# A row-LSTM kernel: 64-row matmul pieces, and gates to output in two parts

## The chip, the cores and the metric

The kernel runs on one core of one Trainium2 chip. The metric is the device time of one launch in microseconds. A profiled execution gives a page and a trace of every instruction; durations below come from it. The engines are called PE or TensorE (matmuls; PEld are its weight loads), DVE or VectorE, ACT or ScalarE, POOL or GpSimd, and SP or SyncE, which here issues all DMAs.

## The reference

The input is x of shape (8, 96, 128, 128): 8 images, 96 channels, 128 rows, 128 pixels in a row. It is group-normalised over 32 groups, and a row LSTM runs over it from the first row to the last. For each row, a masked three-tap convolution of the normalised row and a three-tap convolution of the previous row's h make four gates:

```python
def step(carry, row_in):
    h, c = carry
    ss = conv(h, W_ss, taps=3) + b_ss          # 96 -> 384 channels
    gates = ss + row_in                        # row_in: masked conv of the normalised row
    g5 = gates.reshape(B, 3, 4, Oc, Wd)        # Oc = 32
    f, i, o = (sigmoid(g5[:, :, k].reshape(B, O, Wd)) for k in (0, 1, 2))
    g = tanh(g5[:, :, 3].reshape(B, O, Wd))
    c_new = f * c + i * g
    h_new = o * tanh(c_new)
    return (h_new, c_new), h_new
```

The output is x plus all h. Everything is float32. Row r + 1 needs h of row r, so the 128 rows are a chain.

## The kernel before, in words

**Halves and half-steps.** The 8 images are two halves of four (`NH = 2`, `BH = 4`). A half-step n is one row of one half: `row, s = divmod(n, 2)`, 256 half-steps in all. The two halves alternate, so that one half's gates can be worked on while the other half's matmuls run. A name with ' belongs to half-step n - 1, with + to n + 1, with * to n + 2 and, in the kernel after, with '' to n - 2. S, F and D are named by the half-step whose h they read; what they make is used two half-steps later.

**Even and odd pixels.** A row of 128 pixels is held as 64 even and 64 odd ones (`J = 64`), each with padding. A three-tap convolution makes an even and an odd output from them with four products in place of six: the moving operands are a sum `vs` (S, line 499), a difference `vf` (F, line 503) and a pair of shifted differences `vd` (D, line 507), each 128 partitions x 256 elements (4 images x 64 pixels), made from `hx`. Partitions 0 to 95 of `hx` hold h, 96 to 127 the last 32 normalised input channels. The 64 other input channels come as `xs`, made ahead by GpSimd (`own_image`, lines 297, 315 and 316), and they are stored twice, on partitions 0 to 63 and on 64 to 127.

**Gate tiles.** The 384 output channels are three tiles A, B, C of 128, each in a PSUM bank of 512 elements: the first 256 are one half, the last 256 the other. Tile A's rows 0 to 95 are the forget gate, B's the input gate, C's the output gate; rows 96 to 127 of all three are g. For each tile the products are:

- 1 with vs into the first half, 2 with vf into the second, and the own products P (first half) and Q (second), with xs.
- then `copy` (cp: first half plus bias to SBUF, called m), `even` (lo: first half = m + second half, line 442) and `odd` (hi: second half = m - second half, line 446).
- then 0 with vd into the first half, 3 with vd into the second, and the own product E into the first.

Products 0, 1, 2, 3 contract over 128 rows, P, Q, E over 64. Before the change `own` puts P, Q and E of tile A on the lower 64 rows of the array, of B on the upper, and of C on either by half, so that neighbours can run together.

**Gates.** `tanh` (ta, ACT, line 449) of g's rows, `sigmoid` (si, ACT, line 456), `forget` (fg: f x c, DVE, line 461), `gated` (gt: i x g, line 465), `cell` (ce: line 474), `cell_tanh` (th, ACT, line 479), `output` (ou: o x tanh(c) into hx of the next row, line 486). From hx come S, F (DVE) and D (POOL) for the same half's next row. `residual` (re, POOL, line 525) adds h to x in place.

**Order.** PE, ACT, DVE and POOL are scheduled by hand (`manual_schedule`): each engine runs its instructions in the order in which the program writes them, and waits for others by semaphores. The steady order is the string `PERIOD` with the products `PRODUCTS` in place of X, played by `do` for n = 3 to 255. One half-step has 12 whole products and, in turn, 8 or 10 own ones.

**Blocks.** Rows are loaded in blocks of four. `finish(n)` comes after re': GpSimd's preparation of coming rows (`work`: one `own_image`, and none, one or two images of `normalise_shared`, line 297), and at a block's last row the store of the block and the loads of the block after the next, all on SP's queue. Before the steady part, some 137 us compute the group statistics and the first row.

Of the kernel before, what the change touches and what calls it, by code (L numbers as in the profile page):

```python
# [8 lines left out]
AF = mybir.ActivationFunctionType  # L9
# [12 lines left out]
def kernel(  # L22
# [32 lines left out]
    nc = tc.nc  # L55
    B, C, H, W = x.shape
    P = 128
    NH = 2
    BH = B // NH
# [4 lines left out]
    C2 = 64  # L64
# [21 lines left out]
    wt = [tap[1], wm[:, 0, :], wm[:, 1, :], tap[2]]  # L86
    wo = [wx[:, 0, :], wx[:, 1, :], tap[3]]
# [73 lines left out]
    E = mybir.EngineType  # L161
# [64 lines left out]
    class Scale:  # L226


        def __init__(self, s, lo, hi, banks=None):
            n, self.name = hi - lo, f"{s}_{lo}"  # L230
            self.st, self.rstd, self.nmr = (
                st[s][:, lo:hi], rstd[s][:, :, lo:hi], nmr[s][:, :, lo:hi]
            )


            self.first, at = banks is None, 0 if banks is None else 3 * BH
            self.banks = banks or [bank(f"{name}{self.name}") for name in ("dm", "pv")]
            self.dm, self.pv = (
                own[:, at : at + i * n].rearrange("p (i b) -> p i b", i=i)
                for own, i in zip(self.banks, (3, 2))  # L240
            )
            self.pm = self.dm[:, 1:3, :]
            self.q, self.t, self.minus = (
                const.tile([P, *shape], F32, name=f"{name}{self.name}")
                for name, shape in (("q", [n]), ("t", [2, n]), ("minus", [2, n]))
            )
            for i in range(2):
                self.mm(self.pv[:, i, :], i, eps[:, 0:n], start=self.first and i == 0)
# [107 lines left out]
    last = NT * NH - 1  # L356
    order = {"A": 0, "B": 1, "C": 2}

    def gt(n, s, row, shape=(C, 2 * HB)):
        return g_pool.tile(list(shape), F32, tag=n, name=f"{n}_{s}_{row}")  # L360

    class HalfStep:


        def __init__(self, n):
            self.n, (self.row, self.s) = n, divmod(n, NH)
            self.ps, self.m1, self.moving, self.done, self.gates = {}, {}, {}, set(), None
            self.started, self.images = set(), {}
            self.hx = hx[self.s][self.row // R % 2][:, self.row % R]
            self.xs = xs[self.s][self.row // R % 2][:, self.row % R]  # L370
            self.c = cs[self.s].rearrange("p t b j -> p (t b j)")
# [14 lines left out]
        def mm(self, a, half, weights, rhs, rows=slice(0, P)):  # L386
            self.take_bank(a)
            new = a not in self.started
            self.started.add(a)

            lo, hi = self.images.get(a, (0, BH))
            cols = slice(lo * J, hi * J)
            nc.tensor.matmul(  # L393
                self.ps[a][:, bass.ts(half, HB)][:, cols],
                weights[rows, bass.ts(a, P)],
                rhs[rows, cols],
                start=new,
                stop=False,
                skip_group_check=True,
            )  # L400

        def own(self, a, i):

            low = a == order["A"] or (a == order["C"] and (self.s == 0 or (self.n, i) == (1, 2)))
            rhs = self.xs[:, i].rearrange("p b j -> p (b j)")
            self.mm(a, i % 2, wo[i], rhs, slice(0, C2) if low else slice(C2, P))

        def p_(self, a):
            self.own(a, 0)
# [5 lines left out]
        def t_(self, a):  # L415
            if 2 * self.row + self.s == last:
                self.mm(a, 0, wh, self.xs[:, 2].rearrange("p b j -> p (b j)"))
            else:
                self.own(a, 2)

        def m1_(self, a):
            self.mm(a, 0, wt[1], self.moving["vs"][:, 0])

        def m2_(self, a):
            self.mm(a, 1, wt[2], self.moving["vf"][:, 0])

        def m0_(self, a):
            self.mm(a, 0, wt[0], self.moving["vd"][:, 1])

        def m3_(self, a):  # L430
            self.mm(a, 1, wt[3], self.moving["vd"][:, 0])

        def copy(self, a):
            self.m1[a] = self.tile(f"m{a}", (P, HB))
            m1, column = self.ps[a][:, 0:HB], bias[:, a : a + 1]
            if a == order["A"] and self.n not in (0, 2):
                nc.vector.tensor_scalar(self.m1[a], m1, column, None, ALU.add)
            else:
                nc.scalar.activation(self.m1[a], m1, AF.Identity, bias=column)  # L439

        def even(self, a):
            nc.vector.tensor_add(self.ps[a][:, 0:HB], self.m1[a], self.ps[a][:, HB:])  # L442

        def odd(self, a):
            hi = self.ps[a][:, HB:]
            nc.vector.tensor_sub(hi, self.m1[a], hi)  # L446

        def tanh(self, a):
            nc.scalar.activation(self.g[a * 32 : (a + 1) * 32], self.ps[a][C:P], AF.Tanh)  # L449


        def sigmoid(self, a):
# [7 lines left out]
            if self.row > 0:  # L460
                nc.vector.tensor_mul(f, f, self.c)  # L461

        def gated(self):
            to = self.g if self.row > 0 else self.c
            nc.vector.tensor_mul(to, self.ps[1][0:C], self.g)


        def part(self, ap, lo, hi):
            return ap.rearrange("p (t b j) -> p t b j", t=2, b=BH)[:, :, lo:hi]

        def cell(self, lo=0, hi=BH):
            if self.row > 0:
                c, f, g = (self.part(ap, lo, hi) for ap in (self.c, self.ps[0][0:C], self.g))
                nc.vector.tensor_add(c, f, g)  # L474

        def cell_tanh(self, lo=0, hi=BH):
            if lo == 0:
                self.th = self.tile("th")
            nc.scalar.activation(self.part(self.th, lo, hi), self.part(self.c, lo, hi), AF.Tanh)  # L479

        def output(self, lo=0, hi=BH):
            s, row = self.s, self.row
            nxt = hx[s][(row + 1) // R % 2][0:C, (row + 1) % R]
            self.h = strided(nxt[:, 0, 0, :], 0, [(BH * JP + 1, 2), (JP, BH), (1, J)])
            o, th = (self.part(ap, lo, hi) for ap in (self.ps[2][0:C], self.th))
            nc.vector.tensor_mul(self.h[:, :, lo:hi], o, th)  # L486


        def operand(self, name, parts=1):
# [65 lines left out]
    def work(n):  # L555
        if n < len(FIRST):
            return FIRST[n]
        row, s = divmod(n, NH)
        k, r = divmod(row, R)
        parts = []  # L560
        if r == R - 1 and k + 2 < NB:
            parts.append((own_image, s, k + 2, 0))
        elif r < R - 1 and k + 1 < NB:
            parts.append((own_image, s, k + 1, r + 1))
        if k + 1 < NB:
            parts += shared(s, k + 1, *SHARED[r])
        if r == R - 2 and k + 2 < NB:
            parts.append((load_rows, s, k + 2))
        return parts

    def finish(n):
        for part, *args in work(n):
            part(*args)
        row, s = divmod(n, NH)
        k, r = divmod(row, R)
        if r == R - 1:
            store(s, k, R - 1 if k + 1 == NB else 0, R)
            if k + 2 < NB:
                load(s, k + 2)
        elif r == R - 2 and k + 1 == NB:  # L580
            store(s, k, 0, R - 1)
# [2 lines left out]


    PERIOD = (
        "2A 1A siB' fg' 2B taB' cpA 1B loA 3C' cpB hiA 0C' loB 1C taC' hiB 2C siC' 0A gt'",
        "3A cpC ce' 0B loC th' hiC", "X", "ou' F' S' D' re'", "3B taA siA",
    )
    PRODUCTS = (  # L590
        "P+A P+B Q+A Q+B P+C P*A Q+C EA EB EC",
        "Q+A P+B P+C Q+B Q+C EB EA EC",
    )
    PARTS = {
        "P": "p_", "Q": "q_", "E": "t_", "1": "m1_", "2": "m2_", "0": "m0_", "3": "m3_",
        "cp": "copy", "lo": "even", "hi": "odd", "ta": "tanh", "si": "sigmoid",
# [7 lines left out]
            steps[n] = HalfStep(n)  # L604
        return steps[n]

    def do(n, names):

        for name in names.split():
            at = n  # L610
            for mark, offset in (("'", -1), ("+", 1), ("*", 2)):
                if mark in name:
                    at, name = n + offset, name.replace(mark, "")
            tile_ = name[-1] if name[-1] in order else ""
            part = name[: len(name) - len(tile_)]

            if part in ("S", "F", "D"):
                at += NH
            if not 0 <= at <= last:
                continue  # L620
            step = half_step(at)
            if name not in step.done:
                step.done.add(name)
                getattr(step, PARTS[part])(*([order[tile_]] if tile_ else []))

# [117 lines left out]
    n = m = 0  # L745
    for b in range(B):
# [7 lines left out]
        for k in range(QW // CH):  # L754
# [11 lines left out]
            if alone:  # L766
                i = list(shares).index(k)
# [60 lines left out]
    finish(0)  # L828
    do(1, "gt th 0+A 3+A 0+B 3+B 0+C 3+C ou F S D re")
    finish(1)  # L830
    do(2, "taA siA P+C P*A Q+C")
    for n in range(3, last + 1):
        for names in PERIOD if n < last else PERIOD[:1]:
            do(n, PRODUCTS[n % 2] if names == "X" else names)
            if "re'" in names.split():
                finish(n - 1)
    do(last, "3A EA cpC ce' taA siA 0B 3B EB loC hiC th' siB taB fg ou' re'")
    finish(last - 1)
    do(last, "0C 3C EC taC siC gt")
    step, halves = half_step(last), [(0, BH // 2), (BH // 2, BH)]  # L840
    for at in halves:
        step.cell(*at)
# [60 lines left out]
```

## Time and profile before

| | |
|---|---|
| median of 3 runs | 2062.37 us (2062.25 to 2062.47) |
| span of the profiled execution | 2059.9 us |
| granted TensorE clock, mean | 0.997 |
| MATMUL instructions (two to each float32 product) | 10888 |
| TensorE busy from 160 to 2040 us | 1880.00 of 1880 us |
| VectorE, ScalarE, GpSimd busy in that stretch | 1554.98, 1247.29, 1380.49 us |

A matmul's record lasts longer than its share of the array: records overlap, so the rate is read from start to start. In a line of the timeline the numbers are start and duration in us; a line that ends in x6 holds six instructions of one kind. In the view of waits the numbers are us in total, times, and the longest. In the view of a tile they are ns (least, median, most) and the first and last start in us. The small difference between the median of the runs and the span, 2.5 us, lies around the profiled instructions.

### The profile page before, as it was taken

Reading aid. Unit: us, or ns where it says so; the run is one execution under the profiler, and the core shown is the slowest. Engines: PE = TensorE matmul, PEld = TensorE weight load, DVE = VectorE, ACT = ScalarE, POOL = GpSimd, SP = SyncE. Lnnn points to the kernel's source line nnn. Section 1 sums busy time; section 2 is a strip of 40 time slices with the busy share of each in tenths; the row PEclk is TensorE's granted clock in tenths of the full one; section 3 lists DMA queues with packets and bytes.
Section 4 is the critical chain, followed back from the end, with each engine's and each line's share of the span. In section 5 each row is a group of like instructions: output and inputs, shape, how many; then the busy total and the mean of one; then the engine's idle time right before and its main releaser. Section 6 shows DMA issues by size and latency. Waiting matters only on the chain.

```text
span 2059.9 us, 31445 instructions
## 1 busy us (share of the span) xinstructions
PE 1961.9 (95%) x10888; PEld 1597.5 (78%) x10888; DVE 1675.9 (81%) x3489; ACT 1363.7 (66%) x2403; POOL 1449.6 (70%) x1652
## 2 busy tenths in 40 slices
PE   0399999999999999999999999999999999999998
PEld 0278888888888888888888888888888888888886
DVE  5778888888888888888888888888888888888887
ACT  4776666666666666666666666666666666666666
POOL 3358777777777777777777777777777777777762
PEclk9999999999999999999999999999999999999999
DMA  9994333344433334443333443333444333344411
GB/s 381 424 309 109 91 84 89 97 113 113 107 74 85 88 99 113 113 103 75 86 88 101 113 113 100 73 90 87 104 113 113 99 74 87 88 106 113 113 31 32
DMA packets 103326, 236.26 MB, mean 115 GB/s; under 512 B 5953, under 2 KB 8897, under 8 KB 97281
## 3 DMA queue, kind: packets, MB, share of 16 engines
q1 hardware_dynamic: 103168, 234.25, 41.8%
q8 instruction: 88, 1.44, 0.3%
q14 instruction: 70, 0.57, 0.1%
HBM read 183.90 MB, written 50.33 MB: 114 GB/s over the span
## 4 chain that ended last, share of the span: by engine, by line
PE 93%; DMA 3%; DVE 2%; ACT 1%; POOL 0%; issue 0%; SPq 0%; DVEq 0%; POOLq 0%
PE ps L393 93%; DMA xs<-in_x_dram 3%; DVE bst L771 1%; POOL xw L297 0%; POOL xs L315 0%; POOL xs L316 0%; ACT piece L295 0%; SPq L759 0%; ACT piece L216 0%; ACT xs L216 0%; ACT xs L217 0%; ACT piece L217 0%; ACT g L449 0%; DVE st L677 0%; ACT th L479 0%
## 5 line engine op out<-in xcount | busy, mean ns | idle before, releaser
L393 PE MATMUL ps<-vd,wl 128*128 128x256 f32 x3072 | 814.3, 388 | 0.1
L449 ACT ACTIVATE g<-ps 32x512 f32<-32x512 f32 x768 | 454.3, 592 | 450.5 <-PE ps L393 442.4
L393 PEld LDWEIGHTS ps<-vd,wl 128*128 128x128 f32 x3072 | 562.4, 190 | 151.3 <-issue 84.7
L507 POOL TENSOR_TENSOR vd<-hx 128x512 f32<-128x512 f32 x257 | 266.5, 1037 | 459.0 <-DVE vs L499 457.8
L393 PE MATMUL ps<-xs,wx 64*128 64x256 f32 x3080 | 459.9, 394 | 11.0 <-POOL xs L315 11.0
L393 PE MATMUL ps<-vs,wm 128*128 128x256 f32 x1540 | 460.6, 381 | 4.0 <-POOL vs L499 4.0
L393 PE MATMUL ps<-vf,wm 128*128 128x256 f32 x1540 | 460.4, 381 | 0.0
L456 ACT ACTIVATE ps<-ps 96x512 f32<-96x512 f32 x766 | 417.7, 572 | 16.1
L393 PEld LDWEIGHTS ps<-xs,wx 64*128 64x128 f32 x3080 | 323.9, 187 | 119.7 <-issue 83.9
L461 DVE TENSOR_TENSOR ps<-ps,c 96x512 f32<-96x512 f32 x254 | 176.6, 695 | 259.4 <-ACT ps L456 259.4
L446 DVE TENSOR_TENSOR ps<-m,ps 128x256 f32<-128x256 f32 x768 | 329.1, 429 | 27.3 <-PE ps L393 1.2
L525 POOL TENSOR_TENSOR x<-x,hx 96x512 f32<-96x512 f32 x255 | 330.5, 1296 | 5.7 <-DVE hx L486 5.7
L442 DVE TENSOR_TENSOR ps<-m,ps 128x256 f32<-128x256 f32 x768 | 324.8, 423 | 9.7 <-ACT m L439 0.9
L393 PEld LDWEIGHTS ps<-vs,wm 128*128 128x128 f32 x1540 | 293.6, 191 | 45.9 <-POOL vs L499 5.0
L393 PEld LDWEIGHTS ps<-vf,wm 128*128 128x128 f32 x1540 | 293.9, 191 | 41.1 <-POOL vf L503 0.5
L439 ACT ACTIVATE m<-ps,wl 128x256 f32<-128x256 f32 x514 | 243.9, 475 | 74.8 <-PE ps L393 61.5
L316 POOL TENSOR_TENSOR xs<-xw 128x512 f32<-128x512 f32 (+1 forms) x254 | 270.4, 1064 | 0.0
L393 PE MATMUL ps<-xs,wt 64*128 64x256 f32 x1530 | 264.6, 377 | 0.0
L479 ACT ACTIVATE th<-c 96x512 f32<-96x512 f32 (+1 forms) x257 | 161.4, 628 | 104.8 <-DVE c L474 103.8
L297 POOL TENSOR_SCALAR hx<-x,rstd,nmr 32x512 f32<-32x512 f32 (+1 forms) x252 | 204.7, 812 | 25.9
L297 POOL TENSOR_SCALAR xw<-xr,rstd,nmr 128x512 f32<-128x512 f32 x252 | 204.8, 813 | 8.1 <-DVE nmr L289 6.5
L393 PEld LDWEIGHTS ps<-xs,wt 64*128 64x128 f32 x1530 | 195.0, 187 | 18.1 <-issue 0.7
(91 smaller groups left out, 1295.2 us busy)
## 6 DMA issues: line engine op xcount, KB each, us to landing
xr<-in_x_dram SPq DMA_DIRECT2D x124, 512.0 KB, 6.7
x<-in_x_dram SPq DMA_DIRECT2D x63, 768.0 KB, 5.9
out_dram<-x SPq DMA_DIRECT2D x62, 768.0 KB, 4.9
xs<-in_x_dram SPq DMA_DIRECT2D x30, 1024.0 KB, 12.3
piece<-in_x_dram SPq DMA_DIRECT2D x16, 1024.0 KB, 12.3
x<-in_x_dram SPq DMA_DIRECT2D x62, 256.0 KB, 3.2
xs<-in_x_dram SPq DMA_DIRECT2D x4, 512.0 KB, 8.3
out_dram<-x SPq DMA_DIRECT2D x2, 576.0 KB, 3.8
```

The source lines that it names most:

```text
L297: engine.tensor_scalar(dst, src, scale, shift, ALU.mult, ALU.add)
L316: nc.gpsimd.tensor_sub(differences, strided(xw[:, 0, :], 0, [(W + 1, n), (J, 2), (1, J)]), strided(xw[:, 0, :], J + 1, [(W + 1, n), (0, 2) ...
L393: nc.tensor.matmul(self.ps[a][:, bass.ts(half, HB)][:, cols], weights[rows, bass.ts(a, P)], rhs[rows, cols], start=new, stop=False, skip_g ...
L439: nc.scalar.activation(self.m1[a], m1, AF.Identity, bias=column)
L442: nc.vector.tensor_add(self.ps[a][:, 0:HB], self.m1[a], self.ps[a][:, HB:])
L446: nc.vector.tensor_sub(hi, self.m1[a], hi)
L449: nc.scalar.activation(self.g[a * 32 : (a + 1) * 32], self.ps[a][C:P], AF.Tanh)
L456: nc.scalar.activation(gate, gate, AF.Sigmoid)
L461: nc.vector.tensor_mul(f, f, self.c)
L479: nc.scalar.activation(self.part(self.th, lo, hi), self.part(self.c, lo, hi), AF.Tanh)
L507: diff = nc.gpsimd.tensor_sub(self.operand("vd", 2)[:, :, lo:hi], strided(h, 1, [(BH * JP - 1, 2), (JP, hi - lo), (1, J)]), strided(h, 0, ...
L525: (nc.gpsimd if 2 * row + s < last else nc.vector).tensor_add(xo, xo, self.h)
```

## The change

It has four parts.

1. In the steady part each of the products 0, 1, 2, 3 is issued as two pieces of 64 rows, and P, Q and E as one piece each. `Lanes` gives every piece the lower or the upper 64 rows of the array: the two pieces of a product take different ones, and otherwise the lanes alternate. Where a piece goes to a bank whose last product ran on the other rows, `Lanes.wait` makes TensorE wait first for that product's end. In `PERIOD` a product's name stands twice where it has two pieces.
2. tanh of C, gated, cell, cell_tanh and output are issued in two parts, first the odd pixels (b), then the even ones (a).
3. `PERIOD` and `PRODUCTS` become one string. The copy of tile A goes from VectorE to ScalarE (except in half-steps 1 and 255). D and the residual belong to the half-step two back (''), and `finish` comes with the residual; its GpSimd part is split off as `prepare` and stands at W.
4. The gates of half-step 2 (the second row's first half) are written out ahead of the steady order, which now begins at n = 2. The ending has an order of its own.

```diff
+    OWN = {"P": 0, "Q": 1, "E": 2}
+    class Lanes:
+        ROWS = (slice(0, C2), slice(C2, P))
+        def take(self, first=None):
+            if first is not None:
+                self.last = 1 - self.ROWS.index(first)
+            elif self.taken[0] != self.taken[1]:
+                self.last = int(self.taken[1] < self.taken[0])
+            else:
+                self.last = 1 - self.last
+            self.taken[self.last] += 1
+            return self.ROWS[self.last]
+        def wait(self, number):
+            if number > self.waited:
+                tc.add_manual_dep(
+                    nc.tensor.nop().ins,
+                    self.made[number].ins.name,
...
+                self.waited = number
...
+            before = self.writer.get(a)
+            if before is not None and before[0] != rows and whole not in (before[0], rows):
+                lanes.wait(before[1])
+            made = nc.tensor.matmul(
...
+            self.writer[a] = rows, lanes.issued(made)
...
+        def piece(self, kind, a):
+            if kind in OWN:
+                i, rows = OWN[kind], lanes.take()
+                self.mm(a, i % 2, wo[i], self.xs[:, i].rearrange("p b j -> p (b j)"), rows)
+                return True
+            first = self.halves.pop((kind, a), None)
+            rows = lanes.take(first)
+            half, i, (name, part) = H_PRODUCTS[kind]
+            self.mm(a, half, wt[i], self.moving[name][:, part], rows)
+            if first is None:
+                self.halves[kind, a] = rows
+            return first is not None
...
-            if a == order["A"] and self.n not in (0, 2):
+            if a == order["A"] and self.n in (1, last):
                 nc.vector.tensor_scalar(self.m1[a], m1, column, None, ALU.add)
...
     PERIOD = (
-        "2A 1A siB' fg' 2B taB' cpA 1B loA 3C' cpB hiA 0C' loB 1C taC' hiB 2C siC' 0A gt'",
-        "3A cpC ce' 0B loC th' hiC", "X", "ou' F' S' D' re'", "3B taA siA",
-    )
-    PRODUCTS = (
-        "P+A P+B Q+A Q+B P+C P*A Q+C EA EB EC",
-        "Q+A P+B P+C Q+B Q+C EB EA EC",
-    )
+        "2A hiC' siA' D'' 1B 1A taA' 2B fg' 3C' 1A 0C' re'' taB' 2A 2B EC' 1B cpA 0C' 2C W loA cpB "
+        "3C' 1C siB' loB PB+ QA+ hiA taCb' 2C hiB taCa' 0A gtb' 1C siC' gta' EA 0B ceb' cpC 3A PA+ "
+        "cea' thb' PC+ 3B loC tha' QC+ oub' EB oua' QB+ 3A F' 3B 0A S' 0B"
+    )
+    PIXELS = {"a": (0, BH, 0), "b": (0, BH, 1)}
+    SPLIT = ("taC", "gt", "ce", "th", "ou")
...
-    do(2, "taA siA P+C P*A Q+C")
-    for n in range(3, last + 1):
-        for names in PERIOD if n < last else PERIOD[:1]:
-            do(n, PRODUCTS[n % 2] if names == "X" else names)
-            if "re'" in names.split():
-                finish(n - 1)
-    do(last, "3A EA cpC ce' taA siA 0B 3B EB loC hiC th' siB taB fg ou' re'")
-    finish(last - 1)
-    do(last, "0C 3C EC taC siC gt")
+    do(2, "taA siA taB fg siB taC gt siC ce th ou F S D")
+    for n in range(2, last + 1):
+        do(n, PERIOD, by_lanes=True)
+    do(last, "cpA cpB cpC loA hiA loB hiB loC hiC 0A 3A EA 3B 0B EB", by_lanes=True)
+    do(last, "taA siA 0C 3C EC siB taB fg taC siC gt oua' oub' re'", by_lanes=True)
```

## The prediction

> **What bounds the kernel now.** I read the page first: is one engine full all the time, and is its clock whole?
>
> ```profile
> span 2059.9 us, 31445 instructions
> PE 1961.9 (95%) x10888; PEld 1597.5 (78%) x10888; DVE 1675.9 (81%) x3489; ACT 1363.7 (66%) x2403; POOL 1449.6 (70%) x1652
> PEclk9999999999999999999999999999999999999999
> PE 93%; DMA 3%; DVE 2%; ACT 1%; POOL 0%; issue 0%; SPq 0%; DVEq 0%; POOLq 0%
> ```
>
> TensorE is busy from the 137th microsecond on, the clock is full, and the chain that ended last lies on it for 93%. Whether it waits inside that time is told by the waits (who waited for whom: us in total, times, longest).
>
> ```profile
> POOL vd L507 <- DVE vs L499: 457.8, 249, 5.4
> ACT g L449 <- PE ps L393: 442.4, 506, 3.3
> DVE ps L461 <- ACT ps L456: 259.4, 253, 1.1
> PEld ps L393 <- issue: 169.3, 511, 0.3
> ```
>
> All other engines wait; TensorE waits for none of them in the steady part. But 511 times, twice in each of some 255 half-steps, its weight load stops for 0.33 us with no releaser. The timeline of one half-step shows where:
>
> ```profile
> 1002.60 1.46 PE L393 MATMUL ps<-vd,wl 128*128 128x256 f32 x6
> 1003.98 1.17 PEld L393 LDWEIGHTS ps<-xs,wx 64*128 64x128 f32 x12 [0.33 <-issue]
> 1003.99 1.57 PE L393 MATMUL ps<-xs,wx 64*128 64x256 f32 x12
> 1005.38 0.38 PE L393 MATMUL ps<-xs,wt 64*128 64x256 f32 x1
> 1006.34 0.30 PEld L393 LDWEIGHTS ps<-vd,wl 128*128 128x128 f32 x2 [0.33 <-issue]
> 1006.88 0.59 PE L393 MATMUL ps<-vf,wm 128*128 128x256 f32 x2
> ```
>
> Each float32 product is two MATMULs. Six of 128 rows take 1.46 us, the last record 0.38: one each 0.216 us, 0.432 a product. Twelve of 64 rows come as six pairs, so two 64-row products take the time of one. The sixth 128-row MATMUL leaves the array at 1002.60 + 6 x 0.216 = 1003.90; the seventh pair starts at 1005.38, so the first streamed from 1005.38 - 6 x 0.216 = 1004.09: 0.19 lost between the two shapes. Back again: ten pairs end at 1006.25, the third 128-row one starts at 1006.88, the first at 1006.45: 0.20. The half-step is then (12 + 9/2) x 0.432 + 0.39 = 7.51 us, and the view of the tile vs, one operation a half-step, confirms it:
>
> ```profile
> L499 DVE TENSOR_TENSOR vs<-hx x251: 409/418/1283, 163.4 to 2043.7; 128x256 f32<-128x256 f32 x126
> ```
>
> (2043.7 - 163.4) / 250 = 7.521. So the bound is TensorE, with 0.39 of shape changes in it.
>
> **Pieces of 64 rows.** The 12 whole products become 24 pieces, with 9 own ones 33: 33 / 2 x 0.432 = 7.13, the same array time, and both changes of shape fall away: -0.39. Here a rule speaks against it: the Trainium skill, "TensorE: Matmul & The Clock Gate", part 3, "The mechanism", lets a weight load overlap a running matmul only if the row group differs. Pieces of one lane share theirs; by the rule each pays two loads of about 0.107 us (that page's columns / 1.2 GHz; the trace's own first load after a change costs the same 0.1), so 16.5 x 0.646 = 10.7 us a half-step, some 2,830 us in all. The rows above have it otherwise: six 64-row pairs, load and all, at 0.216. I take the row.
>
> **Waits between lanes.** A piece in a bank that the other row group wrote last waits for that product's end. Writing out lanes for the 33 pieces, a half-step has seven such waits; three are five to seven pieces back and long over, four are three back (second 1A, first EC', second 2C, second 3B). Behind the waiting instruction stand all later pieces of both lanes. The lane waited for has one more piece queued, 0.432, less 0.107 for the next weights: 0.325. The product's record ends 0.16 after its streaming (0.38 - 0.216), so a wait is free while the signal takes up to 0.16, and above that each holds both lanes. No row shows PE waiting for PE. Nearest: DVE to TensorE's load 0.06, and for the upper end VectorE to GpSimd, 0.17 (vs ends 1006.24, vd starts 1006.41).
>
> ```profile
> 149.32 0.65 DVE L503 TENSOR_TENSOR vf<-hx 128x256 f32<-128x256 f32 x1
> 150.03 0.30 PEld L393 LDWEIGHTS ps<-vf,wm 128*128 128x128 f32 x2 [0.40 <-DVE vf L503]
> ```
>
> I take 0.06, as the waiter is the same: nothing. At 0.17 it is 4 x 0.01 = 0.04. The same page's "The cost: per-tile semaphore tail" has increments queue up: estimated at 25 + 2 x 4.7 + 2 x 26.3 = 87 ns for two tiles with one each, which 0.16 still covers.
>
> **Gates in two parts.** tanh of C, gated, cell, its tanh and output go in halves of 256 elements. Rows for halves and for spacing:
>
> ```profile
> 2053.91 0.75 DVE L474 TENSOR_TENSOR c<-ps,g 96x256 f32<-96x256 f32 x2
> 2054.37 0.75 ACT L479 ACTIVATE th<-c 96x256 f32<-96x256 f32 x2 [0.60 <-DVE c L474]
> 1004.76 0.68 DVE L486 TENSOR_TENSOR hx<-ps,th 96x512 f32<-96x512 f32 x1
> 1005.47 0.43 DVE L503 TENSOR_TENSOR vf<-hx 128x256 f32<-128x256 f32 x1
> ```
>
> A half lasts 0.416, and the next independent one starts 0.334 after it; one that needs its predecessor starts 0.03 after its end. VectorE loses the copy of A (0.48) and has fifteen operations: about 6.6 us as before. ScalarE goes from nine to twelve (three copies 0.475, five gates 0.58, four halves 0.41: 6.0 us), below 7.37, so hidden by VectorE's run below: its last tanh half ends 0.1 before output wants it. If that cover is missed, output and all behind it slip by as much.
>
> **The new loop.** With 7.13 of array work the chain from gates to next operands must be looked at, all in one half-step from where 2A streams at 0. 2A, 1A, 3C', 0C', 2B, 1B are one lane: the second 1B leaves at 6 x 0.432 = 2.59, its record ends 2.75. copy of B 2.79 to 3.26. even of B starts 3.30, and VectorE then runs without a gap: odd A, odd B, gated b, a, cell b, a, even C, output b, a: nine starts x 0.336 = 3.02, so output a at 6.32. It ends 6.74; difference (F) 6.78 to 7.21; signal 0.06, load 0.107: next 2A at 7.37. Array work has 0.24 of slack in that. Part of it goes to 0A, which stands behind odd A (3.64 to 4.07, signal and load 4.24) where its lane is free at 3.88: 0.36, with the second 1C, EA and all later pieces queued behind it. The lanes change roles every half-step, so each pays it once in two, 0.18 a half-step: 7.31, still under 7.37, and with nothing to spare for a second such wait. What is late at the end is 2A: TensorE becomes the waiter.
>
> GpSimd delays F once in four half-steps, where two images are normalised:
>
> ```profile
> 417.34 1.71 POOL L297 TENSOR_SCALAR hx<-x,rstd,nmr 32x512 f32<-32x512 f32 x2
> 418.84 0.48 DVE L503 TENSOR_TENSOR vf<-hx 128x256 f32<-128x256 f32 x1
> ```
>
> F begins inside a GpSimd operation and ends 0.27 after that one ends (419.05 to 419.32). From 0.34 on GpSimd needs 1.0 + 1.28 + 2.66 + 2 x 0.9, to 7.0: F ends 7.28, +0.08, over four +0.02. So 7.39.
>
> **Moved steps.** The residual and what finish issues (store, then two loads on SP) come one half-step later, behind shifted (1.04) on GpSimd; normalising moves after them. From residual to the first use of the loaded rows there are about 10 us against 4.9 (store) + 3.2 (load) on the page: hidden, with 2.8 us of vd's slack behind; without it about 1 us x 32 blocks. Second row's gates first: step 2's chain ends about 155.0 instead of 156.5, but step 3's copies stand behind its tanh on ScalarE until 153.5 (151.2 before), so even and odd come around 155.1 to 156.5, fifteen pieces (3.2) follow, and vs of step 5 is at about 166.7, not 163.4: +3.3, between -2 and +6. The last half-step mixes shapes four more times, 4 x 0.195 = +0.8 (0 to 2).
>
> **Sum.** 250 x (7.521 - 7.39) = -32.8, +3.3, +0.8: -28.7. The profiled span becomes 2031; the median of the runs is 2.5 above the span (2062.4), so 2033.
>
> **Rivals.** Array-bound (0.12): if VectorE starts more tightly, or copy B's chain is shorter, 2A waits little and the pace goes to 7.15 to 7.30: 1973 to 2011. For it: 0.24 idle on the array; against: 0.334 is the closest spacing in the trace. Gain mostly given back (0.12): margins of 0.1 (tanh halves before output, copy C before even C) missed one after another, 7.45 to 7.53: 2048 to 2068. For it: ScalarE has three more operations; against: each start was taken from a row. Slower (0.14): the wait between lanes. If a product's signal reaches the next load later than 0.16, each of the four three-back waits holds both lanes: 7.39 + 4 x (l - 0.16). From l = 0.20 it is slower than before; at 0.25, 7.75 and about 2123. For it: no row shows such a wait; against: the longest row for any signal is 0.17. Likeliest (0.62): VectorE's loop, 7.33 to 7.45, 2018 to 2048.
>
> **Numbers.** A measurement tells 0.2%, 4 us, from no change. Faster: 0.62 + 0.12 + over half of the second rival, 0.81; same 0.03; slower 0.14 + 0.02. For 8 in 10 the range takes in the upper part of the array-bound case and the lower part of the slow one: 1998 to 2075.
>
> **What would show it.** Right: no 0.33 us issue gaps in the steady part; tile vs at about 7.39; 2A's load waiting some 0.2 for F; DVE gapless from even B to S. Wrong: loads released by PE (signal above 0.16), VectorE starts wider than 0.34 or idle before output, or no TensorE wait at all.

## The result, and the profile after

The changed kernel takes 2038.71 us (median of four runs, 2038.09 to 2039.03) against 2062.31 us (2062.25 to 2062.47) for the kernel before on the same chip: a ratio of 0.9886, 95% interval 0.9872 to 0.9900. The forecast was 2033 us, faster with a chance of 0.81, range 1998 to 2075. The sign and the mechanism hold; the gain is 23.6 us instead of 29.

The page of the kernel after, its head and its chain:

```profile
span 2036.8 us, 44840 instructions
PE 1935.1 (95%) x16936; PEld 1834.1 (90%) x16936; DVE 1535.7 (75%) x3993; ACT 1494.9 (73%) x3159; POOL 1450.9 (71%) x1652
PEclk9999999999999999999999999999999999999999
PE 92%; DMA 4%; DVE 2%; ACT 1%; POOL 0%; issue 0%; SPq 0%; DVEq 0%; POOLq 0%
```

TensorE issues 6048 more MATMULs (the pieces) and is busy for a little less time. On this page nothing looks like a new bound: TensorE is still at 95%, and the chain still lies on it. The waits of TensorE's weight loads over the whole span (us in total, times, longest) show what went away; the third line is the same wait from 170 to 2015 us, the steady part. The tile vs shows how much it was worth:

```profile
PEld ps L440 <- issue: 18.8, 76, 3.0
PEld ps L440 <- PE ps L440: 2.2, 5, 0.5
PEld ps L440 <- issue: 11.9, 64, 0.2
```

```profile
L571 DVE TENSOR_TENSOR vs<-hx x251: 409/417/1285, 172.3 to 2018.0; 128x256 f32<-128x256 f32 x126
```

The two stops of 0.33 us in each half-step (169.3 us, 511 times before) are gone: in the steady part 64 stops are left, none longer than 0.2 us. Waits of TensorE for its own other lane, the mechanism of the slower rival, are five in the whole execution and none in the steady part. A half-step is (2018.0 - 172.3) / 250 = 7.383 us; it was 7.521, and 7.39 was forecast.

Where the 23.1 us between the two profiled executions (2059.9 and 2036.8) come from follows from the same two lines: start, up to vs of half-step 5: 172.3 - 163.4 = +8.9; steady part: 1845.7 - 1880.3 = -34.6; end, from the last vs: 18.8 (2036.8 - 2018.0) - 16.2 = +2.6. Forecast were +3.3, -32.8 and +0.8. The steady part was a little better than forecast, and the two ends gave back 7.4 us more.

Inside one lane a weight load runs beside the matmul before it, as TensorE's timeline shows for the two MATMULs of one piece with vs:

```profile
1001.26 0.18 PEld L440 LDWEIGHTS ps<-vs,wm 64*128 64x128 f32 x1
1001.44 0.38 PE L440 MATMUL ps<-vs,wm 64*128 64x256 f32 x1
1001.44 0.19 PEld L440 LDWEIGHTS ps<-vs,wm 64*128 64x128 f32 x1
1001.66 0.38 PE L440 MATMUL ps<-vs,wm 64*128 64x256 f32 x1
```

The second load begins with the first MATMUL, and the second MATMUL starts 0.22 after the first, so nothing is added to the 0.216.

The new loop can be read in VectorE's timeline of one half-step of the kernel after (start and duration in us; 2A streams at 1000.17):

```profile
1003.01 0.90 DVE L510 TENSOR_TENSOR ps<-m,ps 128x256 f32<-128x256 f32 x2 [0.70 <-ACT m L506]
1003.81 0.75 DVE L514 TENSOR_TENSOR ps<-m,ps 128x256 f32<-128x256 f32 x2
1004.48 0.74 DVE L535 TENSOR_TENSOR g<-ps,g 96x256 f32<-96x256 f32 x2
1005.14 0.74 DVE L545 TENSOR_TENSOR c<-ps,g 96x256 f32<-96x256 f32 x2
1005.80 0.42 DVE L510 TENSOR_TENSOR ps<-m,ps 128x256 f32<-128x256 f32 x1
1006.13 0.74 DVE L558 TENSOR_TENSOR hx<-ps,th 96x256 f32<-96x256 f32 x2
1006.91 0.58 DVE L575 TENSOR_TENSOR vf<-hx 128x256 f32<-128x256 f32 x1
1007.41 0.41 DVE L571 TENSOR_TENSOR vs<-hx 128x256 f32<-128x256 f32 x1
```

The first row is even A and even B, then come odd A and odd B, gated b and a, cell b and a, even C, output b and a, difference (F), total (S). Each row begins before the one above it has ended, but for F, which needs output a and starts 0.04 after it: VectorE never stands still for longer. Even B starts at 1003.48, 3.31 after 2A; output a at 1006.47, nine starts or 2.99 later. TensorE's weight loads and GpSimd at the end of that half-step:

```profile
1007.27 0.40 PEld L440 LDWEIGHTS ps<-vd,wl 64*128 64x128 f32 x2
1007.54 0.29 PEld L440 LDWEIGHTS ps<-vf,wm 64*128 64x128 f32 x2
```

```profile
1005.48 1.73 POOL L297 TENSOR_SCALAR hx<-x,rstd,nmr 32x512 f32<-32x512 f32 x2
```

The next 2A's load starts at 1007.54, 0.05 after F ends (1006.91 + 0.58): TensorE waits for F, as step "The new loop" had it. The view of waits has no row for it in the steady part, where a load for the other lane (vd, at 1007.27) lies just before; that F sets the pace is shown by the first experiment. And this F takes 0.58 instead of 0.43, because it ends 0.28 after a GpSimd operation that runs to 1005.48 + 1.73 = 1007.21.

### The profile page after: what moved, and what is told of

The parts are those of the page before. It is cut to its first block, busy times and chain, and to the rows that moved or that the text cites. A ratio compares the mean times of both kernels' runs of the same rounds, so it can differ in the third digit from the quotient of the medians.

```text
span 2036.8 us, 44840 instructions
## 1 busy us (share of the span) xinstructions
PE 1935.1 (95%) x16936; PEld 1834.1 (90%) x16936; DVE 1535.7 (75%) x3993; ACT 1494.9 (73%) x3159; POOL 1450.9 (71%) x1652
## 4 chain that ended last, share of the span: by engine, by line
PE 92%; DMA 4%; DVE 2%; ACT 1%; POOL 0%; issue 0%; SPq 0%; DVEq 0%; POOLq 0%
PE ps L440 92%; DMA xs<-in_x_dram 4%; DVE bst L863 1%; ACT g L518 0%; ACT xs L216 0%; ACT xs L217 0%; POOL xw L297 0%; POOL xs L315 0%; POOL xs L316 0%; ACT piece L295 0%; DVE hx L558 0%; SPq L851 0%; DVE g L535 0%; DVE c L545 0%; DVE ps L514 0%
## 5 line engine op out<-in xcount | busy, mean ns | idle before, releaser
L440 PE MATMUL ps<-vd,wl 64*128 64x256 f32 (+1 forms) x6096 | 1392.9, 380 | 2.9 <-DVE ps L514 2.6
L440 PEld LDWEIGHTS ps<-vd,wl 64*128 64x128 f32 (+1 forms) x6096 | 1029.5, 187 | 54.2 <-issue 16.5
L440 PE MATMUL ps<-vs,wm 64*128 64x256 f32 (+1 forms) x3052 | 789.8, 382 | 4.9 <-POOL vs L571 4.0
L440 PE MATMUL ps<-vf,wm 64*128 64x256 f32 (+1 forms) x3052 | 781.9, 380 | 0.0
L440 PE MATMUL ps<-xs,wx 64*128 64x256 f32 x3080 | 643.1, 378 | 11.2 <-POOL xs L315 11.1
L518 ACT ACTIVATE g<-ps 32x256 f32<-32x256 f32 (+1 forms) x1020 | 468.5, 482 | 26.9 <-PE ps L440 6.3
L440 PEld LDWEIGHTS ps<-vf,wm 64*128 64x128 f32 (+1 forms) x3052 | 476.9, 187 | 11.2 <-POOL vf L575 0.5
L440 PEld LDWEIGHTS ps<-vs,wm 64*128 64x128 f32 (+1 forms) x3052 | 452.1, 186 | 24.1 <-POOL vs L571 5.1
L440 PE MATMUL ps<-xs,wt 64*128 64x256 f32 x1530 | 456.7, 379 | 0.1
L535 DVE TENSOR_TENSOR g<-ps,g 96x256 f32<-96x256 f32 (+1 forms) x506 | 188.7, 412 | 4.5 <-ACT g L518 4.5
```

What stands on the lines that cost most here:

```text
L440: made = nc.tensor.matmul(self.ps[a][:, bass.ts(half, HB)][:, cols], weights[rows, bass.ts(a, P)], rhs[rows, cols], start=new, stop=False, ...
L518: nc.scalar.activation(self.part(g, lo, hi, t), self.part(ps, lo, hi, t), AF.Tanh)
L535: nc.vector.tensor_mul(to, i, g)
```

## Experiments

All times are medians; the kernel before is at 2062.2 to 2062.7 us beside each. The half-step of each kernel is worked out as above, from vs of half-step 5 to the last vs.

**VectorE's run sets the pace: one operation more in it, and one outside it.** Two kernels each get one operation with 256 elements in each partition more per half-step, whose output nobody reads: one right behind even B (`XR`, in the diff), the other behind forget, where VectorE has idle time (`fg' XF' 3C'` in the first line of `PERIOD`).

```diff
+        def extra_run(self):
+            nc.vector.tensor_add(scratch, self.m1[1], self.ps[1][:, HB:])
+        def extra_front(self):
+            nc.vector.tensor_mul(scratch[0:C], self.ps[0][0:C, 0:HB], self.m1[1][0:C])
...
-        "3C' 1C siB' loB PB+ QA+ hiA taCb' 2C hiB taCa' 0A gtb' 1C siC' gta' EA 0B ceb' cpC 3A PA+ "
+        "3C' 1C siB' loB XR PB+ QA+ hiA taCb' 2C hiB taCa' 0A gtb' 1C siC' gta' EA 0B ceb' cpC 3A PA+ "
```

> One more VectorE operation of 128x256 per half-step, into a scratch tile that nobody reads, right behind even B, inside the run. Theory (VectorE's run to F sets the pace): +0.34 us a half-step, 250 x 0.34 = +84, about 2123. Rival (lanes and their waits set it, with VectorE busy 75%): 2037 to 2055.

> The same extra work on VectorE, but behind forget, where it waits for the copy of A anyway. Theory (only the run from even B to F counts): 2036 to 2046. Rival (VectorE's whole work sets the pace): the same +84 as for the operation in the run, about 2123.

In the run: 2149.56 us (2148.79 to 2150.80), ratio 1.0423 (1.0407 to 1.0438), half-step 7.819. In front: 2039.26 us (2038.55 to 2039.46), ratio 0.9887 (0.9872 to 0.9902), half-step 7.382. The same kind of operation costs 111 us in one place and 0.6, less than the runs differ among themselves, in the other. So the run from even B to F is the loop, and VectorE's other operations are not. It cost more than 250 x 0.336, 111 us where 84 were expected; VectorE's timeline of the first kernel shows why:

```profile
1007.15 0.90 DVE L511 TENSOR_TENSOR ps<-m,ps 128x256 f32<-128x256 f32 x2 [0.70 <-ACT m L507]
1008.09 0.42 DVE L514 TENSOR_TENSOR scratch<-m,ps 128x256 f32<-128x256 f32 x1
1008.43 0.75 DVE L521 TENSOR_TENSOR ps<-m,ps 128x256 f32<-128x256 f32 x2
```

The extra operation reads the bank that even B writes, and starts 0.04 after even B's end (1007.15 + 0.90), where odd A in the kernel after starts 0.10 before it. It takes 0.46 from the run, not 0.336. The trace's record of the operation holds a wait for VectorE's own semaphore, which VectorE's operations count up, and its start fits a wait for even B's end: the program makes it wait, though it reads only the half that even B does not write.

**An edit that should have shortened the run.** Odd A is moved out of it, to right behind even A, into VectorE's idle time before copy B.

```diff
-        "2A hiC' siA' D'' 1B 1A taA' 2B fg' 3C' 1A 0C' re'' taB' 2A 2B EC' 1B cpA 0C' 2C W loA cpB "
-        "3C' 1C siB' loB PB+ QA+ hiA taCb' 2C hiB taCa' 0A gtb' 1C siC' gta' EA 0B ceb' cpC 3A PA+ "
+        "2A hiC' siA' D'' 1B 1A taA' 2B fg' 3C' 1A 0C' re'' taB' 2A 2B EC' 1B cpA 0C' 2C W loA hiA cpB "
+        "3C' 1C siB' loB PB+ QA+ taCb' 2C hiB taCa' 0A gtb' 1C siC' gta' EA 0B ceb' cpC 3A PA+ "
```

> VectorE's odd A moves ahead of even B, into the gap before the copy of B is there. Theory (the half-step is copy B, even B and nine VectorE starts to F, then the next 2A): the run is one start shorter, so half-steps fall from 7.33 to about 7.23, where the wait of 3B for EB and 33 pieces are the next bound; where two images are normalised F still waits for GpSimd, so 7.29 in the mean: -22 us, 2008 to 2020. Rival (pieces and waits between lanes set the pace, VectorE only follows): unchanged, 2037 to 2040.

Measured: 2047.71 us (2047.15 to 2050.40), ratio 0.9928 (0.9911 to 0.9944), half-step 7.423. That is 9 us slower than the kernel after, where a gain of 19 to 31 was expected. VectorE's and ScalarE's timelines of this kernel:

```profile
1002.40 0.43 DVE L510 TENSOR_TENSOR ps<-m,ps 128x256 f32<-128x256 f32 x1 [0.78 <-ACT m L506]
1002.87 0.43 DVE L514 TENSOR_TENSOR ps<-m,ps 128x256 f32<-128x256 f32 x1
1003.20 0.42 DVE L510 TENSOR_TENSOR ps<-m,ps 128x256 f32<-128x256 f32 x1
1003.66 0.43 DVE L514 TENSOR_TENSOR ps<-m,ps 128x256 f32<-128x256 f32 x1
```

```profile
1001.90 1.00 ACT L506 ACTIVATE m<-ps,wl 128x256 f32<-128x256 f32 x2 [0.39 <-PE ps L440]
```

Copy A starts at 1001.90, which is 0.04 after the end of the second 2A, though it reads only the half that 1A writes (1A's second piece had ended at 1001.43). The record of the copy holds a wait for TensorE's semaphore, and 2A's last MATMUL counts that up where 1A's does not: the program makes the copy wait for the last product in the bank, whichever half it goes to. So even A starts at 1002.40, odd A after it, on the same bank and with a wait for VectorE's semaphore, at 1002.87, and even B at 1003.20, where its copy, over at 1002.90, would have let it start 0.27 earlier. The run has lost one start (-0.336), but even B comes later (+0.27), and odd B now stands directly behind even B, on the same bank, at 0.46 in place of 0.336 (+0.12). Together about +0.05 a half-step; measured are 7.423 - 7.383 = 0.04. The order of the change, even A, even B, odd A, odd B, keeps neighbours on different banks.

**Gates in two parts undone.** tanh of C, gated, cell, its tanh and output are whole again, all else as in the kernel after.

```diff
-        "3C' 1C siB' loB PB+ QA+ hiA taCb' 2C hiB taCa' 0A gtb' 1C siC' gta' EA 0B ceb' cpC 3A PA+ "
-        "cea' thb' PC+ 3B loC tha' QC+ oub' EB oua' QB+ 3A F' 3B 0A S' 0B"
+        "3C' 1C siB' loB PB+ QA+ hiA taC' 2C hiB 0A 1C siC' gt' EA 0B cpC 3A PA+ "
+        "ce' PC+ 3B th' loC QC+ EB ou' QB+ 3A F' 3B 0A S' 0B"
```

> Undoes the second part alone: tanh of C, gated, cell, its tanh and output are whole again, the pieces and the rest of the order stay. Theory (chain from the last products of C to F): gated waits for the whole tanh of C (about 4.3 after 2A), cell starts 0.72 later, its tanh ends 6.4, output 7.1, F 7.55, next 2A at 7.72 in place of 7.37: +0.35 a half-step, +87, about 2125, more than before the change. Rival (the halves add operations and hide nothing, as gated starts at the same time): 2030 to 2045.

2149.16 us (2148.15 to 2150.12), ratio 1.0418 (1.0403 to 1.0434), half-step 7.824: +0.44, where +0.35 was expected. Without the halves the pieces do not make the kernel faster than before but slower. VectorE's timeline:

```profile
1006.10 0.95 DVE L510 TENSOR_TENSOR ps<-m,ps 128x256 f32<-128x256 f32 x2 [1.11 <-ACT m L506]
1006.96 0.76 DVE L514 TENSOR_TENSOR ps<-m,ps 128x256 f32<-128x256 f32 x2
1007.72 0.69 DVE L535 TENSOR_TENSOR g<-ps,g 96x512 f32<-96x512 f32 x1
1008.44 0.69 DVE L545 TENSOR_TENSOR c<-ps,g 96x512 f32<-96x512 f32 x1
1009.04 0.42 DVE L510 TENSOR_TENSOR ps<-m,ps 128x256 f32<-128x256 f32 x1
1009.82 0.69 DVE L558 TENSOR_TENSOR hx<-ps,th 96x512 f32<-96x512 f32 x1 [0.36 <-ACT th L550]
1010.61 0.43 DVE L575 TENSOR_TENSOR vf<-hx 128x256 f32<-128x256 f32 x1
```

From odd A to F are 3.65 us here and 3.10 in the kernel after. cell waits for gated's end (0.72 apart where two halves need 0.66), and VectorE stands still for 0.36 before output, until the whole tanh is done. Whether the pieces would gain in the old order, without the rest of the change, no run here tests.

**GpSimd's share.** `normalise_shared` prepares one image in every half-step instead of one, one, two and none.

```diff
-    SHARED = ((0,), (1,), (2, 3), ())
+    SHARED = ((0,), (1,), (2,), (3,))
```

> GpSimd's normalising is spread, one image after each of four rows in place of one, one, two, none. In the changed kernel the two half-steps of eight with two images take 7.47 and 7.45, the others 7.33 to 7.39, and there F ends 0.27 after a GpSimd operation that it overlaps. Theory (F waits for GpSimd's operation to end): all eight come to 7.33 to 7.35, -0.04 in the mean, -11, about 2028. Rival (the longer half-steps come from the loads and stores at the block's end): unchanged, 2037 to 2040.

2031.47 us (2030.93 to 2032.78), ratio 0.9849 (0.9834 to 0.9863), half-step 7.357. The mean half-steps by their place in a block of eight are, in order, 7.384, 7.336, 7.334, 7.333, 7.335, 7.474, 7.453, 7.388 in the kernel after and 7.417, 7.311, five of 7.33, 7.422 here: the two long ones (7.474 and 7.453) are gone, and F takes 0.42 there; in return two others, at the ends of the row, grow to 7.42. The undisturbed pace is 7.33.

**TensorE's pieces undone.** Every product is whole again, in the new order and with the gates in two parts.

```diff
-            if by_lanes and (part in OWN or part in H_PRODUCTS) and (
+            if False and (part in OWN or part in H_PRODUCTS) and (
```

> The new order and the gates in two parts, but every product whole again, as before the change: 128 rows for 0, 1, 2, 3 and 64 for P, Q, E. Theory (TensorE's array time and shape changes bound the kernel, and the pieces took them away): in the new order P, Q and E stand singly between whole products, so none runs beside another: (12 + 9) x 0.432 = 9.07 us of array, and up to some six places with a change to and fro, 0.39 each less what is neighbours: about 10.1 us a half-step, 2038.7 + 250 x (10.1 - 7.38) = about 2720 us; 2460 if shape changes cost nothing. Rival (VectorE's loop bounds the new order whatever the shape): 2040 to 2060.

2739.45 us in one run; half-step (2718.3 - 175.0) / 250 = 10.173. The view of waits, from 200 to 2700 us:

```profile
PEld ps L440 <- issue: 733.5, 2212, 0.3
DVE ps L510 <- ACT m L506: 695.0, 246, 2.8
```

Nine stops of 0.33 us in each of the 246 half-steps, where the old order had two, and VectorE idle for 2.8 us of each half-step. The new order puts 64-row and 128-row products side by side, so in this kernel it is worth nothing until all have one shape. The count in the expectation was right in sum, not in its parts: the timeline has ten changes of shape (1.95 us), and some own products do find a partner.

**Waits between lanes.** The second piece of 2C is put right behind the first 1C, its neighbour in the bank on the other lane, so that one wait has no cover.

```diff
-        "3C' 1C siB' loB PB+ QA+ hiA taCb' 2C hiB taCa' 0A gtb' 1C siC' gta' EA 0B ceb' cpC 3A PA+ "
+        "3C' 1C 2C siB' loB PB+ QA+ hiA taCb' hiB taCa' 0A gtb' 1C siC' gta' EA 0B ceb' cpC 3A PA+ "
```

> The second piece of 2C comes right behind the first 1C, which it has to wait for: a wait one piece back in place of three. Theory (a wait holds the pieces of both lanes behind it, and is free only while the other lane has a piece queued as cover): the product's end and 0.06 of signal and the weight load are now open on one lane by 0.43, on the other by 0.33, and the last pieces of C behind it come later by as much: +0.30 a half-step, +74, about 2112. Rival (a wait costs its own lane alone, which has slack): 2037 to 2050.

2108.19 us (2106.94 to 2110.89), ratio 1.0221 (1.0206 to 1.0237), half-step (2088.2 - 171.9) / 250 = 7.665. Its view of waits, and the loads at the place:

```profile
PEld ps L440 <- PE ps L440: 110.1, 240, 0.5
```

```profile
1003.67 0.19 PEld L440 LDWEIGHTS ps<-vs,wm 64*128 64x128 f32 x1
1004.31 0.18 PEld L440 LDWEIGHTS ps<-vf,wm 64*128 64x128 f32 x1 [0.46 <-PE ps L440]
1004.32 0.18 PEld L440 LDWEIGHTS ps<-xs,wx 64*128 64x128 f32 x1
```

A single wait without cover stops the weight loads for 0.46 us and holds both lanes (the load of xs for the other lane comes 0.01 behind); the half-step is longer by 7.665 - 7.383 = 0.28, and the kernel is slower than before by 2.2%. So the slower rival was a real mechanism; in the change's order it doesn't happen, because at three pieces back the signal of 0.06 us fits into the cover of 0.16. In the kernel after the second 2C shows this: 1C's record ends at 1003.80 and 2C's load is at 1003.86.

**The start.** The line that plays the second row's gates ahead of the steady order is taken out.

```diff
-    do(2, "taA siA taB fg siB taC gt siC ce th ou F S D")
```

> Undoes the fourth part alone: the second row's gates are not written out ahead, the steady order makes them. In the changed kernel vs of step 5 starts at 172.3 us, not at 163.4 as before; TensorE stands idle for 2.65 us from 153.9 on, and its clock is granted at 0.50 from there to 163.3. Theory (the gates ahead leave TensorE without work, and the clock falls): no idle stretch of over 2 us, no half clock after 150 us, vs of step 5 at about 164.5, and some 8 us less than the changed kernel, about 2031. Rival (the steady order itself starts slowly, whoever makes the second row's gates): 2037 to 2040.

2032.67 us (2031.79 to 2033.36), ratio 0.9855 (0.9841 to 0.9870), with vs of half-step 5 at 166.4. So this part of the change costs 6.0 us (172.3 - 166.4 = 5.9 in the profiles). The windows view of the kernel after (columns: stretch, its length, PE, PEld, DVE, ACT and POOL busy with numbers of instructions, granted clock, DMA share, GB/s) and TensorE's timeline show what else happened:

```profile
153.95:156.95 3.00, 0.35 (x2) 0.03 (x1) 2.96 (x7) 0.32 (x1) 2.24 (x3) 0.87 1.07 214
157.00:160.00 3.00, 3.00 (x11) 2.51 (x13) 0.57 (x3) 0.47 (x1) 2.81 (x4) 0.50 0.30 60
160.00:163.30 3.30, 3.30 (x17) 2.43 (x13) 0.43 (x1) 0.00 (x0) 3.12 (x4) 0.55 0.00 0
156.20:163.00 6.80, 6.05 (x25) 5.03 (x26) 1.79 (x5) 0.47 (x1) 6.43 (x8) 0.50 0.26 52
163.30:172.30 9.00, 8.84 (x66) 7.52 (x66) 4.97 (x14) 5.49 (x12) 3.48 (x5) 1.00 0.54 118
```

```profile
153.71 0.59 PE L440 MATMUL ps<-vf,wm 64*128 64x256 f32 x2
156.95 1.19 PE L440 MATMUL ps<-vd,wl 64*128 64x256 f32 x2 [2.65 <-DVE ps L514]
```

TensorE is idle for 2.65 us, from 154.30 on, until VectorE has done the first odd A behind half-step 2's gates, F and S. Inside this gap the granted clock falls to 0.5; it stays there from 156.2 to 163.0, and a MATMUL's record lasts 0.63 us instead of 0.38. In the kernel before the clock is 1.00 from 149 to 180 us. How long the half clock lasts differs between executions: after the same gap (2.64) it was 3.4 us in the kernels with one image, with the wait one back and with the last pieces, and from VectorE's first vs to vs of half-step 5 these took 33.8 to 34.0 us, where the kernel after took 35.3. The Trainium skill, "TensorE: Matmul & The Clock Gate", "Why this matters for your kernels", advises to leave TensorE no idle gap longer than about 3 us, since the clock falls to half; here 2.65 us were enough. Two things could make the start late, then: the order itself, and the clock. The next kernel keeps the order and fills the gap with five products of 128 rows that nobody reads, in the bank that half-step 4's tile C starts anew.

```diff
+            if name == "Z":
+                if n == 3:
+                    unread = half_step(n + 1)
+                    unread.take_bank(order["C"])
+                    for _ in range(5):
+                        nc.tensor.matmul(
+                            unread.ps[order["C"]][:, 0:HB],
+                            wt[0][:, 0:P],
+                            wt[0][:, 0:HB],
...
-        "3C' 1C siB' loB PB+ QA+ hiA taCb' 2C hiB taCa' 0A gtb' 1C siC' gta' EA 0B ceb' cpC 3A PA+ "
+        "3C' 1C siB' loB PB+ QA+ hiA taCb' 2C hiB taCa' Z 0A gtb' 1C siC' gta' EA 0B ceb' cpC 3A PA+ "
```

> Five products of 128 rows without a reader (2.2 us) are put on TensorE in its idle stretch before the first odd A of half-step 3 (154 to 157 us), into the bank that half-step 4's tile C will overwrite. Theory (the idle stretch makes TensorE run at half clock from 157 to 163.3, which loses half of 6.3 us): clock 1.0 there, the operand vs of half-step 5 starts at about 169.1 instead of 172.3, and the time falls by 3.2 to about 2035.5 us. Rival (the start is late because ScalarE and VectorE do the second row's gates first; the clock hides behind it): no change, 2038.7, or a little more.

2035.51 us (2035.30 to 2036.11), ratio 0.9870 (0.9853 to 0.9886). Its windows:

```profile
153.95:156.95 3.00, 3.00 (x14) 2.20 (x13) 2.96 (x6) 0.67 (x2) 2.17 (x3) 1.00 1.06 209
157.00:160.00 3.00, 2.70 (x21) 2.50 (x22) 1.49 (x4) 0.47 (x1) 2.92 (x4) 1.00 0.67 137
160.00:163.30 3.30, 3.16 (x26) 2.41 (x23) 0.51 (x1) 1.69 (x3) 3.02 (x5) 1.00 0.00 0
```

The clock stays at 1.00, and work without any use makes the kernel 3.2 us faster. vs of half-step 5 is at 169.8. What lies ahead of VectorE's first vs (at 137.1 us in the kernel before, 137.0 after, 137.3 here, 137.0 without the early gates) is not part of the change, so I count from there to vs of half-step 5: 26.30, 35.33, 32.50 and 29.45 us. That splits the start into three: 35.33 - 32.50 = 2.83 for the half clock, 32.50 - 29.45 = 3.05 for the gates' place in the order, and 29.45 - 26.30 = 3.15 that stay without the early gates.

**The end.** The last half-step's products are pieces too.

```diff
-                at < last or part in ("P", "Q") or (part, order[tile_]) in step.halves
+                True
...
-    do(last, "taA siA 0C 3C EC siB taB fg taC siC gt oua' oub' re'", by_lanes=True)
+    do(last, "taA siA 0C 3C EC 0C 3C siB taB fg taC siC gt oua' oub' re'", by_lanes=True)
```

> The last half-step's products are 64-row pieces too. In the changed kernel 18.8 us lie between the last vs and the end (16.2 before), with five changes of shape between. Theory (these changes are most of the 2.6): about 2 us less, 2036 to 2037.5. Rival (the order of the ending is what is longer): 2038 to 2040.

2036.69 us (2036.15 to 2037.13), ratio 0.9872 (0.9856 to 0.9889): 2.0 less, as expected, but hardly for the expected reason. From the last vs to the end are 2035.3 - 2016.9 = 18.4 us, only 0.4 less than in the kernel after; most of the difference lies in the steady stretch (half-step 7.379 against 7.383: 1 us), which the edit doesn't touch, and is near what runs of one kernel differ by. The waits of TensorE from the last vs on, in the kernel after and then in this one:

```profile
PEld ps L440 <- PE ps L440: 0.9, 2, 0.5
```

```profile
PEld ps L440 <- PE ps L440: 2.8, 6, 0.5
```

Changes of shape were traded for waits between lanes: the own products of a following half-step, which elsewhere stand between the pieces, are not there.

**The three gains together.** No gates ahead, one image in each half-step, pieces to the end.

> Three edits together: the second row's gates no longer ahead of the steady order, one image normalised in each half-step, and pieces in the last half-step too. If the three gains have separate causes they add: 2038.7 - 6.0 - 7.2 - 2.0 = 2023.5 us, with the half-step at 7.35 and no stretch at half clock after 150 us. If they share a cause (if, say, the start or the end waits on the same GpSimd work that the images move), the sum falls short: 2026 to 2032.

2027.42 us (2027.31 to 2028.82), ratio 0.9831 (0.9816 to 0.9846), half-step (2006.9 - 167.5) / 250 = 7.358: the fastest kernel here, 11.3 us below the kernel after, but 3.9 short of the plain sum. In the traces the three gains add all the same. From the first vs to vs of half-step 5 are 29.47 us (29.45 without the early gates alone), a half-step is 7.358 (7.357 with one image alone), and the end 18.4 (18.4 with the last pieces alone). It is the plain sum that was too large: the 2.0 of the last experiment were only 0.4 in the end itself, the 7.2 of the one image only 6.5 in the steady part, and the first vs, ahead of everything that was changed, starts at 138.0 here instead of 137.0. No shared cause is needed, and none shows.

## Why the prediction was right, and where it was off

**Shape changes and pieces: right.** The stops of 0.33 us are gone, and the weight loads of one lane run beside its matmuls: 7.383 leaves no room for the 10.7 of the rule weighed there (in all some 2,850 us by its own terms, not 2,830), and the row was the better guide. Undoing the pieces alone puts the kernel at 2739 us.

**Waits between lanes: right, free.** Signal 0.06, as taken from DVE to TensorE; no visible wait in the steady part. The kernel with one uncovered wait shows that the price is a stop of 0.46, and that the margin, not luck in the count, decided it.

**The new loop: right, 7.383 for 7.39.** Forecast and measured, from 2A's streaming: even B +3.30 and +3.31, nine starts 3.02 and 2.99, 2A 0.05 after F's end. That it came so close is in part luck, for two sizes inside were off and cancel. The undisturbed half-step is 7.33, not 7.37. And GpSimd's delay of F costs 0.12 to 0.14 in two half-steps of eight, not 0.08: the step's terms (0.34 + 1.0 + 1.28 + 2.66 + 1.8) add up to 7.08, not to its 7.0, and would have given 0.14 to 0.15. Two neighbours of the long half-steps are longer as well, at 7.384 and 7.388; their cause stays open. The margins for tanh halves and copy C (the rival with the gain given back) held: VectorE has no gap in the run.

**Gates in two parts: necessary.** The step said that halves follow each other at 0.334. They do, also where both read one bank (gated b and a start 0.33 apart). Where the program makes an operation wait for the one before it, because that one writes to the same bank, it is 0.46. The change's order keeps such pairs apart, and so the forecast, which did not know of it, came out right: luck in this point. The expectation for odd A moved forward did not, and missed by 28 to 40 us.

**Moved steps: the step that was mis-sized.** The residual and what `finish` issues are hidden, as said: in the steady part no engine but SP waits for a DMA. "Second row's gates first" put vs of step 5 at 166.7, "+3.3, between -2 and +6"; it came at 172.3, +8.9 and outside that range. The gates' place in the order is 3.05 of it, about the +3.3 that the step reckoned with. The half clock is 2.83; the step left it out, although by its own times, even and odd at 155.1 to 156.5, TensorE has nothing to do before them. (They ran from 155.7 to 157.1: F, just before, took 1.17 us beside GpSimd.) A further 3.15 belong to none of the steps. They are not work of the new order laid earlier: counted in MATMULs of 64 rows, with one of 128 rows as two, TensorE starts 202 between the first vs and vs of step 5 in the kernel before and 201 in the one without the early gates (those of 256 columns). So the array is not full there, although TensorE counts as busy (9.19 of the 9.20 us between vs of half-steps 4 and 5). One wait is in sight, vs of half-step 4, which took 1.29 us instead of 0.42 beside GpSimd; for the rest the cause stays open.

**The end: mis-sized, +2.6 for +0.8.** From the last vs to TensorE's last product are 11.4 us, 8.6 before. By the timeline, twelve MATMULs of 64 rows stand there without a partner, at least 0.216 each, between whole products, and two waits between lanes take 0.9; the step counted only four changes of shape. Eight of the twelve are these:

```profile
2020.66 1.45 PE L440 MATMUL ps<-vd,wl 64*128 64x256 f32 x4
2022.16 0.70 PE L440 MATMUL ps<-xs,wt 64*128 64x256 f32 x2
2022.70 0.59 PE L440 MATMUL ps<-vd,wl 64*128 64x256 f32 x2
```

The pieces to the end did not settle how much is due to each.

Sum: with 7.383 for 7.39 (-34.6), the start at +8.9 and the end at +2.6 it is -23.1, the measured difference. Both misses lie outside the loop, where a trace has one instance of each event and no average. Part 3 was not undone alone: what the copy on ScalarE and the later D and residual are worth, no run here shows.

## What to carry to other kernels

When the loop is in the order of a chain, shape every matmul alike first: in this kernel pieces of one shape kept the rate of whole products and left the order free for the chain. Then check each wait's cover in pieces (three back was free here, one back stopped both lanes for 0.46 us), and do not put an operation on VectorE right behind one that writes to the same PSUM bank. At the seams, look for TensorE idle for some 2.6 us: filling such a gap with useless products gained 3 us here.

## What was not expected of the hardware

- An idle stretch of 2.65 us inside full work put TensorE's clock to 0.5 for 6.8 us, and for 3.4 us in three other executions; with five useless products in it the clock stayed at 1.00.
- F, with both inputs in SBUF, took 0.58 instead of 0.43 us where GpSimd ran, and ended 0.28 after the GpSimd operation. The Trainium skill, "SBUF — State Buffer", "SBUF: two separate sides", has VectorE and GpSimd hold a shared port pair as an exclusive lock; the row agrees with that.

Two things that look like the chip's are waits of the program. Two VectorE operations of 256 elements start 0.336 us apart, but 0.46 apart when the second uses the bank that the first writes, though it reads nothing of what was written; and a copy on ScalarE that reads one half of a bank started only 0.04 after the last product into the other half, 0.47 after the end of the products that it reads. The records of both hold a wait for a semaphore. Whether they could start earlier without it, no run here shows.
